# A graph network on one core: how far the upper half of the edges runs ahead of the lower half (LEAD 6 to 10)

## The chip, the cores and the metric

The kernel runs on one core of one Trainium2 chip. The metric is the device time of one execution in microseconds (us); the median of several runs is compared. Besides it there is a profile of one execution: a page of tables, and a trace that can be asked for single instructions.

The engines are named as the profile names them: PE (TensorE, matmuls; PEld is its weight loads), DVE (VectorE), ACT (ScalarE), POOL (GpSimd, which here issues the gathers) and SP (SyncE, which issues most other transfers).

## The reference

Two graph layers, each wrapped in a residual and a layer norm. The inputs are `x` of 6250 nodes x 256 features, and 100000 edges with source `src`, destination `dst` (sorted, and denser at low nodes, as it is 6250 u² for uniform u) and one of 8 types.

```python
# relational convolution, three times (L = 3)
for l in range(3):
    xr  = einsum('nd,rde->rne', x, W_rel[l])          # 8 types
    agg = segment_sum(xr[edge_type, src], dst)        # sum over the edges into a node
    x   = relu(agg + x @ W_root[l] + bias[l])
x = layernorm(x0 + x)
# attention over 4 heads of 64; only the first 6250 edges' weights reach the output
xt    = (x @ weight).reshape(-1, 4, 64)
alpha = softmax(leaky_relu(<xt[src], attn_l> + <xt[dst], attn_r>, 0.01), over heads)
tmp   = sum over heads of alpha[:n] * xt[dst[:n]]
out   = layernorm(x + tmp repeated for the 4 heads)
```

## The kernel before

**Tiles.** Edges are cut into 782 edge tiles of 128, nodes into 49 node tiles of 128. Edge tiles 0 to 35, the edges of the hottest 16 nodes, are handled by counting and by products of their own (`count`, `products`). Edge tiles 36 to 781 are taken in groups of up to four (`GT`), from high numbers to low: 188 groups per layer, 746 edge tiles.

**One group.** For each edge tile, POOL gathers 128 source rows from the table in memory into a message buffer (`gather`, line 499; pool `mp`, eight buffers, tile `msg`). DVE builds a one-hot of type and destination within a small window (`onehot`, line 483, four groups ahead). TensorE multiplies messages by the one-hot (`windows`, line 516, into the tile `pw`), and DVE adds the result into a sum `S` at a place read at run time (`add`, line 528). So `S` holds, for each node and type, the sum of source features.

**Node tiles.** When no later group reaches a node tile, its sums are final: `fold` wraps the ring's rim, `dense` multiplies by the weights (2 matmuls at line 580 and 16 at line 584, 6 matmuls after each group's windows, more where two tiles wait), `finish` (lines 598 to 619) adds the bias and writes the row of the next layer's table; in the third layer it adds the residual, normalizes and writes `y`. `clear` (line 593) zeroes the sums. In the third layer `logits` (line 632, copy at 634) follows two iterations after a finish.

**Two fronts.** Groups are split at edge tile 410 (`TM`). The upper half has a ring `S[0]` of four node tiles, the lower half `S[1]` of three, so that while one half's node tile is in its dense work, the other half's sums can be added. `Plan.order` merges both halves into one list, upper and lower in turn, with now and then two upper groups in a row, and a run of only lower groups at the end; `LEAD` sets how many. Node tile 13 is reached from both halves: its lower part is kept in `hold`, and added at line 827 when the upper half gets there.

**The order of everything.** The three layers are written under a manual schedule: each engine's queue has the order in which `layer` emits. The body of its loop over places in the list (shortened, a yield's worth of each helper at a time):

```python
for i in range(NG + 5):
    # prep step, counting, products, loads of rows for later node tiles
    msg = gather(i); vals = places(i); ohs.append(onehot(i + AHEAD))
    # logits of two iterations ago, finish and clear of node tiles just done
    wins = windows(i, msg, ohs.pop(0))
    # up to 6 dense matmuls per waiting node tile
    add(i, wins, vals)
    # second half of the prep step, transposes of rows, fold of node tiles just reached
```

In the third layer the attention's preparation (`prepare`, lines 723 to 758) begins at place 164 and takes one step for each lower group, and for each iteration after the last group. A step loads indices into a message buffer (line 723), compares the ones loaded before (line 730), builds a mask in another message buffer (line 736), and multiplies, selects and reduces (lines 745, 754, 758).

The next layer's gathers read the table that `finish` writes, so they wait for its last row.

Of the kernel before, what the change touches and what calls it, by code (L numbers as in the profile page):

```python
# [34 lines left out]
PIECE = 6  # L35
WB = 32
AHEAD = 4
LEAD = 6
GWIN = 256
GK = 8  # L40
GCW = 512
# [2 lines left out]
class Plan:  # L44
# [35 lines left out]
    def order(self):  # L80
# [3 lines left out]
        b = [[t for t in k if t < self.TM] for k in g if k[0] < self.TM]  # L84
        n = max(1, len(b) - LEAD)
        seq, k = [], 0
# [1289 lines left out]
```

## Time and profile before

| | us |
|---|---|
| median of 3 runs | 2975.68 |
| lowest and highest | 2972.78, 2980.37 |
| the profiled execution | 2972.97 |
| its span, first to last instruction | 2971.1 |
| mean granted TensorE clock | 0.939 of full |
| busy: PE, POOL, DVE, ACT | 2667.1, 2139.6, 1669.1, 458.5 |

An entry of the groups of instructions reads: line, engine, operation, output <- inputs, count | busy time and mean nanoseconds of one | idle time of the engine just before them, and what ended most of it. "issue" is time in which an engine waited for nothing that the profile shows. An entry of the waits reads: engine, line it stood before <- what it waited for: total us, times, longest us. An entry of the timeline reads: start in us from the span's start, duration in us, engine, line, operation, out <- in, how many instructions were merged, and in brackets the idle time before and what ended it. Matmuls in 32-bit floats appear as two records each.

### The profile page before, as it was taken

What the parts mean: (1) busy time and instruction counts of PE and PEld (TensorE: products, weight loads), DVE (VectorE), ACT (ScalarE), POOL (GpSimd) and SP (SyncE); (2) the same over time, 40 slices, a digit from 0 to 9 for tenths busy, and PEclk for the clock granted to TensorE, in tenths of its full rate; (3) what the DMA queues carried; (4) which work ended last, traced back from release to release, by engine and by line L of the source; (5) the groups of instructions that cost most, each with busy time, mean ns of one, the idle gap of its engine ahead of it and who ended that gap; (6) DMA issues with size and microseconds to landing.
All of it is one profiled execution on the core that took longest, in us unless ns stands there. A gap on an engine that the chain in (4) does not pass through costs nothing.

```text
span 2971.1 us, 45283 instructions
## 1 busy us (share of the span) xinstructions
PE 2667.1 (90%) x15710; PEld 2424.1 (82%) x15711; DVE 1669.1 (56%) x4094; ACT 458.5 (15%) x602; POOL 2139.6 (72%) x2254
## 2 busy tenths in 40 slices
PE   5999999989888799999988988779999999999985
PEld 4989888888777688998878877678888888888874
DVE  7645677764433555555444444356556665554778
ACT  2111111111001111111111110111111111110114
POOL 6777777777775777777777777577777777777741
PEclk9999999999988899999999997799999999998895
DMA  4444444445433444444444543344444444454534
GB/s 153 124 124 122 120 123 119 121 134 156 149 116 95 138 125 122 125 123 118 121 119 138 174 125 115 119 122 127 130 126 128 123 127 128 141 175 139 164 124 165
DMA packets 203053, 388.97 MB, mean 131 GB/s; under 512 B 42885, under 2 KB 128004, under 8 KB 202820
## 3 DMA queue, kind: packets, MB, share of 16 engines
q0 software_dynamic: 107424, 293.48, 33.8%
q1 hardware_dynamic: 92200, 89.76, 9.3%
q10 hardware_dynamic: 3196, 2.76, 0.3%
q8 instruction: 130, 2.13, 0.3%
q14 instruction: 103, 0.84, 0.1%
HBM read 360.18 MB, written 25.65 MB: 130 GB/s over the span
## 4 chain that ended last, share of the span: by engine, by line
PE 69%; POOL 9%; issue 7%; DVE 7%; DMA 5%; ACT 2%; DVEq 0%; ACTq 0%; POOLq 0%
PE pd L584 30%; PE pw L516 30%; POOL msg L499 9%; PE pd L580 4%; DMA msg<-x,idx 3%; DVE S L528 3%; DMA msg<-in_x_dram,idx 2%; PE pd L688 1%; PE pt L632 1%; PE pt L551 1%; ACT xT L554 1%; PE pd L659 1%; DVE st L1032 0%; DVE z L1020 0%; DVE oh L483 0%
## 5 line engine op out<-in xcount | busy, mean ns | idle before, releaser
L499 POOL DMA_INDIRECT msg<-x,idx x1492 | 1418.6, 951 | 504.8 <-issue 410.9
L516 PE MATMUL pw<-oh,msg 128*128 128x160 f32 (+22 forms) x8952 | 1304.7, 303 | 195.8 <-DMA msg<-x,idx 95.7
L516 PEld LDWEIGHTS pw<-oh,msg 128*128 128x128 f32 x8952 | 1248.4, 202 | 263.2 <-issue 104.6
L528 DVE TENSOR_TENSOR S<-S,pw 128x320 f32 (+22 forms) x2238 | 905.1, 404 | 986.7 <-PE pd L584 509.8
L584 PE MATMUL pd<-wr,S 128*128 128x256 f32 x4704 | 1106.7, 386 | 1.7 <-DVE S L528 1.4
L584 PEld LDWEIGHTS pd<-wr,S 128*128 128x128 f32 x4704 | 895.8, 194 | 116.8 <-DVE S L528 3.6
L499 POOL DMA_INDIRECT msg<-in_x_dram,idx x746 | 709.5, 951 | 236.2 <-issue 209.6
L483 DVE TENSOR_TENSOR oh<-iota,key 128x640 f32<-128x640 f32 (+23 forms) x564 | 364.0, 647 | 26.6 <-issue 15.3
L593 ACT ACTIVATE S<-S 128x2048 uint32<-128x2048 uint32 x150 | 285.1, 1900 | 0.1
L554 ACT COPY xT<-pt 128x256 f32<-128x256 f32 x195 | 72.2, 370 | 981.7 <-PE pt L551 969.7
L601 ACT ACTIVATE h<-pd 128x256 f32<-128x256 f32 x98 | 37.6, 383 | 929.8 <-DVE pd L598 747.8
L580 PE MATMUL pd<-wo,xT 128*128 128x256 f32 x588 | 168.8, 413 | 3.3 <-ACT h L601 3.3
L598 DVE TENSOR_TENSOR pd<-pd,bias_b 128x256 f32<-128x256 f32 x147 | 63.1, 430 | 172.5 <-PE pd L584 172.5
L580 PEld LDWEIGHTS pd<-wo,xT 128*128 128x128 f32 x588 | 110.3, 205 | 12.9 <-ACT h L601 3.7
L650 DVE TENSOR_SCALAR sel<-iota,hk 128x392 bf16<-128x392 f32 x138 | 80.4, 613 | 0.0
L615 ACT ACTIVATE rs<-mv,eps 128x1 f32<-128x1 f32 x49 | 14.4, 295 | 414.8 <-DVE mv L614 414.8
L688 PE MATMUL pd<-msg,A 128*128 128x256 f32 x294 | 73.0, 392 | 1.7 <-DMA msg<-x 1.7
L688 PEld LDWEIGHTS pd<-msg,A 128*128 128x128 f32 x294 | 57.0, 201 | 9.0 <-issue 2.1
L551 PE MATMUL pt<-ident,xin 128*128 128x128 f32 x294 | 57.8, 279 | 1.4 <-ACT xT L554 1.4
L632 PEld LDWEIGHTS pt<-w1x,xT 128*128 128x128 f32 x192 | 26.3, 198 | 35.4 <-ACT xT L554 35.4
L551 PEld LDWEIGHTS pt<-ident,xin 128*128 128x128 f32 x294 | 41.5, 146 | 12.6 <-ACT xT L554 2.4
L632 PE MATMUL pt<-w1x,xT 128*128 128x4 f32 x192 | 30.4, 264 | 23.6 <-ACT xT L554 23.6
(187 smaller groups left out, 641.9 us busy)
## 6 DMA issues: line engine op xcount, KB each, us to landing
msg<-x,idx POOLq DMA_INDIRECT x1492
x<-h SPq DMA_DIRECT2D x96, 128.0 KB
xin<-x SPq DMA_DIRECT2D x96, 128.0 KB
msg<-x SPq DMA_DIRECT2D x24, 512.0 KB
msg<-in_x_dram,idx POOLq DMA_INDIRECT x746
y<-yt SPq DMA_DIRECT2D x49, 128.0 KB
xin<-in_x_dram SPq DMA_DIRECT2D x48, 128.0 KB
msg<-in_x_dram SPq DMA_DIRECT2D x12, 512.0 KB
```

Of the source, the lines that this page charges most:

```text
L483: nc.vector.tensor_tensor(oh[:, :len(g), :w], iota[:, :w].unsqueeze(1).to_broadcast([P, len(g), w]), key[:, g[0]:g[-1] + 1].unsqueeze(2).t ...
L499: nc.gpsimd.indirect_dma_start(out=msg[:, q, :], out_offset=None, in_=table, in_offset=bass.IndirectOffsetOnAxis(ap=idx[:, t:t + 1], axis=0))
L516: nc.tensor.matmul(pw[:, k * w:(k + 1) * w], msg[:, q, k * P:(k + 1) * P], oh[:, q, :w], start=True, stop=True)
L528: ins = nc.vector.tensor_tensor(o, o, pw.rearrange("p (a b) -> p a b", b=W), ALU.add)
L551: nc.tensor.transpose(pt[:, k * P:(k + 1) * P], t[:, k * P:(k + 1) * P], ident)
L554: nc.scalar.copy(xT.rearrange("p k n -> p (k n)"), pt[:, :D])
L580: nc.tensor.matmul(pd[:, :D], xT[:, k], wo[:, k], start=(k == 0), stop=False)
L584: i = nc.tensor.matmul(pd[:, :D], s[:, k * R + r], wr[:, k, r], start=False, stop=(k == KC - 1 and r == R - 1))
L593: i = nc.scalar.memzero(cols(f, j))
L632: nc.tensor.matmul(pt[:, :H], yT[:, k], w1x[:, k, D + H:D + 2 * H], start=(k == 0), stop=(k == KC - 1))
L650: nc.vector.tensor_scalar(oh, iota[:, :NT * R], float(512 * n), hk[:, t:t + 1], op0=ALU.add, op1=ALU.is_equal)
L688: nc.tensor.matmul(ph[:, :D], A[:, j], t[:, n], start=(n == 0), stop=(j == js[-1]))
```

## The change

The constant `LEAD` goes from 6 to 10. In `Plan.order` it is subtracted from the number of lower groups to give the stretch over which the upper groups are spread.

```diff
 WB = 32
 AHEAD = 4
-LEAD = 6
+LEAD = 10
 GWIN = 256
```

## The prediction

> **What bounds the kernel now.** I read the page first: busy shares and the chain of waits.
>
> ```profile
> PE 2667.1 (90%) x15710; PEld 2424.1 (82%) x15711; DVE 1669.1 (56%) x4094; ACT 458.5 (15%) x602; POOL 2139.6 (72%) x2254
> PE 69%; POOL 9%; issue 7%; DVE 7%; DMA 5%; ACT 2%; DVEq 0%; ACTq 0%; POOLq 0%
> L499 POOL DMA_INDIRECT msg<-x,idx x1492 | 1418.6, 951 | 504.8 <-issue 410.9
> ```
>
> This looks like TensorE. The waits, and POOL's timeline at the end of the second layer, say otherwise:
>
> ```profile
> POOL msg L499 <- issue: 620.5, 2036, 0.6
> POOL msg L499 <- PE pw L516: 44.5, 109, 3.5
> ```
>
> ```profile
> 1897.61 0.94 POOL L499 DMA_INDIRECT msg<-x,idx  x1 [0.30 <-issue]
> 1898.86 0.95 POOL L499 DMA_INDIRECT msg<-x,idx  x1 [0.30 <-issue]
> 1918.16 0.95 POOL L499 DMA_INDIRECT msg<-x,idx  x1 [18.35 <-DMA x<-h]
> ```
>
> Nearly every gather follows the last by 1.25 us: 0.95 of work and 0.30 that waits for nothing. That gap doesn't count as busy, so "72%" hides a POOL with no free time. A layer has 746 gathers, 746 x 1.25 = 932.5 us. From first start to last end the timeline gives 936.5 (11.14 to 947.61), 934.8 (964.99 to 1899.81) and 952.9 (1918.16 to 2871.06). So layers one and two run at POOL's pace, 5.0 us for a group of four, with 4.0 and 2.3 us lost; layer three loses 20.4 us.
>
> Subtracting 5.0 us per group from the starts in layer three places that loss: 6.4 us at groups 63 to 84, 1.1 at group 144, 11.4 at groups 168 to 187, the rest in crumbs. Five of the gathers concerned:
>
> ```profile
> 2231.60 0.94 POOL L499 DMA_INDIRECT msg<-x,idx  x1 [2.85 <-PE pw L516]
> 2243.23 0.94 POOL L499 DMA_INDIRECT msg<-x,idx  x1 [1.71 <-PE pw L516]
> ...
> 2842.85 0.94 POOL L499 DMA_INDIRECT msg<-x,idx  x1 [1.97 <-PE pw L516]
> ...
> 2846.60 3.08 POOL L499 DMA_INDIRECT msg<-x,idx  x1 [0.30 <-issue]
> ...
> 2866.36 0.95 POOL L499 DMA_INDIRECT msg<-x,idx  x1 [1.62 <-DVE ga L758]
> ```
>
> The first two are a TensorE backlog that fills all eight message buffers. The others lie where the attention's preparation (L723 to L758) takes message buffers too; the 3.08 us gather overlaps the 2.29 us addition at L827.
>
> Between layers POOL idles 17.37 and 18.35 us, since the table must be written. The end of layer two on TensorE:
>
> ```profile
> 1900.80 2.84 PE L584 MATMUL pd<-wr,S 128*128 128x256 f32 x12
> 1903.48 1.87 PE L516 MATMUL pw<-oh,msg 128*128 128x32 f32 x16
> ...
> 1906.43 7.17 PE L584 MATMUL pd<-wr,S 128*128 128x256 f32 x32
> ```
>
> The last windows could start when the last gather has landed. For that I take a group at the start of layer two in the chain: gather start 982.75, windows 986.87, so 4.12 us. 1898.86 + 4.12 = 1902.98, and they start at 1903.48, 0.5 us late, behind dense work of node tile 13.
>
> **What the Trainium skill says.** "Perfetto Trace Analysis", Identifying the Most-Contended Engine: matmul busy time is a bad measure of the bound. The trace agrees: TensorE is 90% busy in layers that POOL paces. Same page, DMA Instruction — SWDGE (GPSIMD): such a slice ends with descriptor generation, not with the data. The trace agrees: 0.95 us of slice, 4.12 us to use. Same page, Optimization Strategy: repeated gaps on the engine that should be saturated can mean too few buffers; that fits POOL's waits in layer three. "SBUF — State Buffer", Who interferes with whom, infers that a two-input tensor_tensor leaves descriptor generation alone. Here the trace differs: the gather that meets L827 takes 2.71, 2.73 and 3.08 us in the three layers, instead of 0.95.
>
> **The change, part by part.** LEAD is used only in the order of groups, whose walk gives both lists. Nothing is added or removed: 94 upper and 94 lower groups, the same instructions, the same three-tile and four-tile rings. What moves: doubled upper groups rise from 5 places to 9; the last upper group goes from place 181 to 177; a run of lower groups closes the layer, 182 to 187 before, 178 to 187 after. SP's row loads, stores and the preparation's loads move with their iterations; rows are asked for three iterations (15 us) before they are turned, the preparation's one step before use. Weight loads stay at the layer's start. Semaphore waits stay where their instructions are.
>
> (1) *Gathers.* 746 per layer at 1.25 us in either order: 0 us. Not hidden by anything, merely unchanged.
>
> (2) *Ends of layers one and two.* Dense work of tiles 14 and 13 ends four iterations earlier, so nothing stands ahead of the last windows: -0.5 us in layer two, and -0.4 in layer one by the same sum (946.67 + 4.12 = 950.79 against 951.22). The rest of the 17 to 18 us is a chain through tile 0 that stays. Bounds: 0 and -1 each.
>
> (3) *TensorE ahead of POOL, layer three.* An upper tile costs 36 dense records of 0.217 us (12 in 2.6 us), a window record is 0.11 to 0.17 us by width, and logits add about 1.7 us per tile. Doubling upper groups earlier brings their dense work earlier. Summed over both lists, TensorE has up to 4.7 us more to do by places 56 to 71, 2.3 on average, and up to 5.6 by places 76 to 92; the lists agree again at the end. Buffers are full there (the 6.4 us), so POOL pays: I take +3 us, between average and first peak. Upper bound +5.6; lower -1.1 (all extra work falls into slack and the wait at group 144 goes). In layers one and two no such wait appears in POOL's timeline, thus 0; what hides the work is buffers not yet full. Without that cover they would pay up to 5.6 each.
>
> (4) *Preparation, layer three.* It takes 15 steps, one per lower group from place 164: nine in the alternation and six at 182 to 187 before; seven and eight (178 to 185) after. While a step both loads and selects, an iteration takes three message buffers; four such iterations follow each other before, six after. VectorE then sets the pace: its L730 starts at 2848.68, 2853.69, 2858.73 are 5.0 us apart, and 7.3 with a finished upper tile. Counting from the preparation's start (2761.72): before, place 178's step starts 69.0 us later and tile 0's dense work 119.0 us later (2880.70). After: 69.0 for the same fourteen iterations, 2.3 for L827, now ahead of 178, 25.2 + 2.3 for the five steps 178 to 182 with tile 14's finish, then the gathers of 185 to 187, 15.0, landing 2.9 (4.12 less 1.25), windows 1.9, and 0.6 of semaphores and addition: 119.2. The lighter 186 and 187 give back what the run costs: 0 us. Bounds: -4 (POOL's waits at 182, 183 and 187 all vanish: 0.73 + 1.69 + 1.32) and +8 (the slower rival).
>
> (5) *The end of layer three.* Tile 0's dense work ends at 2887.87, but VectorE finishes it only at 2889.33, because tile 13's logits (L632, then the copy at L634) come first. After the change those are done by place 185: -1.4 us. Bounds 0 and -1.5. The attention stage handles six late tiles in either order (0, 13 to 17 before; 0, 1, 13 to 16 after): 0 us.
>
> Sum: -0.9 + 3 + 0 - 1.4 = +0.7 us. The profiled execution took 2972.97 us (span 2971.1), which becomes 2973.7; the median of the runs is 2.7 above it, so I forecast 2975.68 + 0.7 = 2976.4 us.
>
> **The rivals.** *Slower: six three-buffer iterations in a row.* If POOL reaches place 178 less than two groups (10 us) ahead of its windows, each gather waits for a whole trip of the group two before: gathers 5.0, landing 2.9, windows 1.9, additions 1.0, select and reduce 2.9, together 13.7, or 6.85 us per group. For it: groups 182 to 183 and 183 to 184 are 6.69 and 7.13 us apart. Against: the next two are 5.03. Six at +1.85 are 11.1, and a second finish inside the run adds 2.3, against 5.1 lost there now: +8.3, with the +0.7 about +9: 2985 us.
>
> *Faster: TensorE is the bound after all.* Then 30 of the 36 dense matmuls of tiles 14 and 13 (60 x 0.217 = 13.0 us) leave each layer's last six groups: -39 us, 2937 us. For it: the chain is 69% PE. Against: POOL's unbroken 1.25 us rhythm, and only 0.5 us of lateness at the last windows. *Faster, by less:* the 11.4 us at groups 168 to 187 all go, since fewer steps lie in the alternation; with steps 2 and 5, -13.7, so 2962 us. Against: step 4's tighter run.
>
> That the change does nothing is excluded by the lists; that it moves nothing measurable is my forecast.
>
> **How the numbers follow.** About 0.3%, 8.9 us, is what a measurement can tell from no change. Forecast 0.80, slower rival 0.14, the faster ones 0.02 and 0.04. The steps' bounds, were all to fall one way, lie 9 below and 13 above the forecast; I hold the range at 2968 to 2988 us, which takes in the slower rival and leaves out the faster ones and the last microsecond of those stacks.
>
> **What would show it.** Right: first to last gather still about 936, 935 and 950 to 958 us; no POOL wait over 1 us in the first two layers; the boundary idles at 17 and 18 us; L827's long gather four groups earlier; larger TensorE waits near groups 56 to 72 of layer three; tile 0's finish directly after its dense work. Wrong: POOL waits in layers one or two, a run from 178 on paced at 6.5 us or more per group, or boundary idles that shrink by several microseconds.

## The result, and the profile after

The change makes the kernel slower. The median of five runs is 3003.9 us (2995.2 to 3005.9), against 2972.8 us (2967.4 to 2980.4) for five runs of the kernel before on the same chip. The ratio on record is 1.0093, with a 95% interval of 1.0077 to 1.0109 (the quotient of the two medians is 1.0105). The forecast was 2976.4 us and the range ended at 2988, so the prediction was wrong. The profiled execution of the kernel after has a span of 3002.1 us, 31.0 longer than before.

The page after, busy time and chain of waits:

```profile
PE 2687.1 (90%) x15710; PEld 2436.1 (81%) x15711; DVE 1667.3 (56%) x4094; ACT 458.0 (15%) x602; POOL 2136.3 (71%) x2254
PE 67%; POOL 10%; issue 8%; DVE 8%; DMA 5%; ACT 2%; DVEq 0%; SPq 0%; ACTq 0%; POOLq 0%
```

The instruction counts are those of before, record for record. Yet PE is busy 20.0 us longer (2667.1 before): the same matmuls ran more slowly. Nothing else on these lines says where.

POOL's timeline does. These are the last gather of layer two and the first of layer three, after:

```profile
1898.64 0.94 POOL L499 DMA_INDIRECT msg<-x,idx  x1 [0.30 <-issue]
1917.71 0.94 POOL L499 DMA_INDIRECT msg<-x,idx  x1 [18.13 <-DMA x<-h]
```

Layer three's first gather starts 0.45 us earlier than before (1917.71 against 1918.16). From there to the last gather:

| stretch of POOL's timeline, us | before | after |
|---|---|---|
| layer one, first to last gather | 936.5 | 935.6 |
| idle to layer two | 17.37 | 18.50 |
| layer two | 934.8 | 934.2 |
| idle to layer three | 18.35 | 18.13 |
| layer three | 952.9 | 986.5 |
| last gather to the end of the span | 100.0 | 97.8 |

All of the loss is in layer three, +33.6 us. The waits there, from the view of waits over 1915 to 2910 us of the kernel after (line, what it waited for: total, times, longest):

```profile
POOL msg L499 <- PE pw L516: 53.3, 52, 4.8
...
POOL msg L499 <- PE pt L551: 12.3, 8, 6.4
PE pd L688 <- DMA msg<-x: 9.4, 4, 2.7
```

In the same view of the kernel before:

```profile
POOL msg L499 <- PE pw L516: 24.7, 44, 3.5
```

POOL's waits for message buffers, which TensorE frees, more than double. The last line of the first fence is the one to follow. It says that TensorE itself waited, four times, in front of a matmul at line 688. That is in `products`, the separate treatment of the 16 hottest nodes, which the prediction didn't mention.

The groups of instructions of the page have the same line. First before, then after:

```profile
L688 PE MATMUL pd<-msg,A 128*128 128x256 f32 x294 | 73.0, 392 | 1.7 <-DMA msg<-x 1.7
```

```profile
L688 PE MATMUL pd<-msg,A 128*128 128x256 f32 x294 | 79.9, 418 | 21.2 <-DMA msg<-x 13.9
```

Same 294 records, 6.9 us more busy time, and 21.2 instead of 1.7 us of idle time ahead of them. These lines are of all three layers: 9.4 of the 21.2 us lie in layer three, the other 11.8 in layers one and two, which became no longer. So a wait here doesn't cost time by itself; why it does in layer three is taken up below.

How the matmuls slow down shows in the windows over 2520 to 2760 us of layer three (stretch, length, busy time and records of PE, PEld, DVE, ACT and POOL, granted TensorE clock, DMA share, GB/s), before and then after:

```profile
2520.00:2760.00 240.00, 224.53 (x1371) 204.59 (x1371) 130.41 (x347) 30.65 (x44) 180.66 (x192) 0.96 0.50 152
```

```profile
2520.00:2760.00 240.00, 214.88 (x1250) 193.41 (x1250) 122.08 (x321) 27.93 (x40) 169.48 (x180) 0.91 0.47 142
```

In the same 240 us POOL issues 180 gathers instead of 192: twelve fewer at 1.25 us are 15 us, near half of layer three's loss. TensorE starts 121 fewer records, is idle 9.7 us more, and its clock is 0.91 instead of 0.96.

### The profile page after: what moved, and what is told of

The parts are those of the page before. It is cut to its first block, busy times and chain, and to the rows that moved or that the text cites. A ratio compares the mean times of both kernels' runs of the same rounds, so it can differ in the third digit from the quotient of the medians.

```text
span 3002.1 us, 45291 instructions
## 1 busy us (share of the span) xinstructions
PE 2687.1 (90%) x15710; PEld 2436.1 (81%) x15711; DVE 1667.3 (56%) x4094; ACT 458.0 (15%) x602; POOL 2136.3 (71%) x2254
## 3 DMA queue, kind: packets, MB, share of 16 engines
q0 software_dynamic: 107424, 293.48, 34.1%
## 4 chain that ended last, share of the span: by engine, by line
PE 67%; POOL 10%; issue 8%; DVE 8%; DMA 5%; ACT 2%; DVEq 0%; SPq 0%; ACTq 0%; POOLq 0%
PE pw L516 30%; PE pd L584 28%; POOL msg L499 10%; PE pd L580 4%; DMA msg<-x,idx 3%; DVE S L528 3%; PE pd L688 2%; PE pt L551 1%; PE pt L632 1%; ACT xT L554 1%; DMA msg<-in_x_dram 1%; DVE sel L650 1%; DVE oh L483 0%; DMA msg<-x 0%; DVE st L1032 0%
## 5 line engine op out<-in xcount | busy, mean ns | idle before, releaser
L580 PEld LDWEIGHTS pd<-wo,xT 128*128 128x128 f32 x588 | 110.7, 205 | 14.7 <-ACT h L601 5.2
L688 PE MATMUL pd<-msg,A 128*128 128x256 f32 x294 | 79.9, 418 | 21.2 <-DMA msg<-x 13.9
L688 PEld LDWEIGHTS pd<-msg,A 128*128 128x128 f32 x294 | 60.0, 209 | 32.1 <-issue 10.8
```

The source lines that it names most:

```text
L580: nc.tensor.matmul(pd[:, :D], xT[:, k], wo[:, k], start=(k == 0), stop=False)
L688: nc.tensor.matmul(ph[:, :D], A[:, j], t[:, n], start=(n == 0), stop=(j == js[-1]))
```

## The late loads: how a change of order reaches them

`products` works in places too: at one place it emits a load of table rows (line 678, on SP's queue), at the next the matmuls that use it (line 688). `finish` puts the store of `y` (line 619) on the same queue, and that store waits until VectorE has normalized the row. This is SP's timeline of the kernel before, at the first such load, and the matmuls that use it:

```profile
2580.12 0.32 SPq L619 DMA_DIRECT2D y<-yt  x1
...
2581.21 0.37 SPq L678 DMA_DIRECT2D msg<-x  x1
```

```profile
2594.91 1.89 PE L688 MATMUL pd<-msg,A 128*128 128x256 f32 x8
```

The load goes out 13.7 us ahead of its use. Here too a store stands ahead of it, but that of the finish at place 126, four places earlier, so that TensorE still has the work of those places to do. After the change the finish is at place 129 and the load at 130 (SP, then PE):

```profile
2605.07 0.32 SPq L619 DMA_DIRECT2D y<-yt  x1
2605.75 0.92 SPq L678 DMA_DIRECT2D msg<-x  x2
```

```profile
2605.46 2.00 PE L516 MATMUL pw<-oh,msg 128*128 128x64 f32 x16 [0.82 <-DVE S L528]
2610.18 3.31 PE L688 MATMUL pd<-msg,A 128*128 128x256 f32 x8 [2.72 <-DMA msg<-x]
...
2621.31 1.89 PE L688 MATMUL pd<-msg,A 128*128 128x256 f32 x8
```

The load is held until the store has gone, and goes out 4.4 us ahead of the matmuls, for which TensorE stands idle 2.72 us. SP's own waits over 2560 to 2760 us tell the store from a lack of message buffers:

```profile
SPq L619 <- DVE yt L618: 141.1, 7, 26.4
...
SPq L678 <- PE pw L516: 1.2, 4, 0.5
```

The stores wait for VectorE, up to 26.4 us; the loads themselves wait hardly at all for TensorE to free a buffer.

After the wait the eight records take 3.31 us instead of 1.89. The Trainium skill, "TensorE: Matmul & The Clock Gate", Part 1: The HAM clock gate, says that an array that falls idle is throttled, and that sustained activity releases it; it puts the idle window at about 3.4 us. In this trace the granted clock is 1.00 over 2605.0 to 2610.1 us and 0.50 over 2612.0 to 2613.5, after a wait of 2.72 us, shorter than that window.

I call a load *late* if the order puts it directly behind a `finish` of the place before. With `LEAD` 6 one of the 13 loads is late (its matmuls are at place 139); with 10 there are four (matmuls at 131, 137, 145, 149). Before, TensorE waits at line 688 once, for 1.7 us; after, four times, for 9.4 us. The count and the waits don't pair off one to one. The wait before belongs to the last load, which has a line of its own (676), since VectorE must clear the rest of its buffer first; after the change it is there again, with 2.0 us. The late load of before is in time. Of the four after, that of 145 is in time too, and the other three are waited for, as the view of line 678 over 2500 to 2800 us has it under "who waited for it":

```profile
  PE pd L688: 7.4, 3
```

In layers one and two `finish` writes no `y`, but it stores the row `h` of the next table (line 602) on the same queue, and that store waits for ScalarE. The order there is the same, so the same loads are late. Layer one after the change, SP and then PE:

```profile
666.25 0.32 SPq L602 DMA_DIRECT2D x<-h  x1
666.75 1.10 SPq L678 DMA_DIRECT2D msg<-in_x_dram  x2
```

```profile
672.82 3.75 PE L688 MATMUL pd<-msg,A 128*128 128x256 f32 x8 [3.64 <-DMA msg<-in_x_dram]
```

At line 688 TensorE waits 7.3 us in layer one and 4.5 in layer two, and neither layer takes longer. The difference is how far behind TensorE is. Taking a group's gathers as usable 4.12 us after the start of its last one, as in the prediction, TensorE begins the windows of place 160 only 0.5 and 0.6 us later than that in layers one and two before the change, but 10.6 us later in layer three.

## The experiments

**Theory S** (late loads): the loss comes from TensorE's waits for loads held behind `y` stores. **Theory M** (message buffers): it comes from POOL, since `products` takes buffers of the ring from the gathers while TensorE is behind. **Theory R** (ratchet): each double upper group costs POOL a wait that is never won back, and they come earlier and larger. Ratios below are to the kernel before, with 95% intervals. The expectations name two rivals more: D, that double upper groups cost the same in every layer, and B, that TensorE's backlog alone is to blame, wherever it is paid. The table gives POOL's waits in layer three by place in the order, in us beyond 5.0 per group:

| places | before | after | own rows | moved products, LEAD 10 | early doubles |
|---|---|---|---|---|---|
| below 48 | 0.3 | 0 | 0.6 | 0 | 0.5 |
| 48 to 95 | 6.8 | 17.6 | 13.7 | 17.8 | 15.9 |
| 96 to 129 | 0.6 | 0.2 | 0.4 | 0.4 | 0.4 |
| 130 to 157 | 1.1 | 16.0 | 0.5 | 1.9 | 0 |
| 158 to 187 | 11.4 | 19.9 | 34.1 | 13.7 | 7.1 |
| sum | 20.2 | 53.7 | 49.3 | 33.8 | 23.9 |

Each column is one execution. Two kernels below repeat an order in layer three: `LEADS` (10, 10, 6) that of before, with 5.5, 6.8 and 13.4 us in the rows 48 to 95, 130 to 157 and 158 to 187, and (6, 6, 10) that of after, with 14.7, 18.0 and 19.0. So a difference of up to some 6 us in a row can be chance.

Eight kernels ran where the kernel before takes 3594 to 3599 us (*slow readings* below): POOL's gathers there show 199 to 225 us of waits whose releaser the trace doesn't name, and layer three can't be read. Six were run again where the kernel before takes some 2975 us; the two that were not stay open.

**Which layers.** `order` takes `lead`, and is called in each layer.

```diff
-LEAD = 6
+LEADS = (10, 10, 6)
```

> LEAD 10 in layers one and two, LEAD 6 in layer three. Theory M (message buffers): the whole loss of about 31 us lies in layer three, where TensorE is close to POOL's pace and other work takes message buffers; so this run is the kernel before again: 2971 to 2976 us, ratio 0.999 to 1.001, layer spans from first to last gather 935, 935 and 953 us. Theory S (SP's queue: product loads held behind the y stores) says the same, as y stores exist only in layer three. Rival D (doubled upper groups cost the same in every layer): 20 us of the 31 stay, 2993 us.

Measured: 2975.02 us, 1.0002 (0.9993 to 1.0011). With `LEADS = (6, 6, 10)`:

> LEAD 6 in layers one and two, LEAD 10 in layer three. Theories M and S: nearly all of the loss, 3001 to 3005 us, layer three 986 us from first to last gather. Rival D: a third of it, about 2983 us.

Measured: 3000.49 us, 1.0081 (1.0058 to 1.0104), four waits of TensorE for the products' loads in layer three, 9.0 us. In the first of the two kernels TensorE waits 8.7 and 4.3 us for such loads in layers one and two, and the run takes no longer. The loss is layer three's alone.

**Between.**

```diff
-LEAD = 6
+LEAD = 8
```

> LEAD 8 in all layers: seven doubled upper groups instead of five and nine, a last run of eight lower groups. Theory M, by a walk of TensorE's work: the excess ahead of places 56 to 72 and 120 to 134 is between those of 6 and 10, so 2980 to 2992 us. Theory S: it depends on whether a finish stands right ahead of place 130, so either near 2973 or near 2990, with no order in the three values. Rival D: half of the loss, 2988 us.

Measured: 2982.92 us, 1.0028 (1.0017 to 1.0039). That is in M's range, and what theory S expected, a time near one of the two ends and no order, did not come. Three loads are late by the count, and TensorE waits for these three, 3.5 us; but the profiled execution took 2976.98 us, the least of the ten, so its waits may be less than usual.

**Products with buffers of their own.** On `LEAD` 10; the room comes from one buffer of the one-hots.

```diff
-            t = mp.tile([P, GT, D], F32, name="msg")
+            t = hp.tile([P, GT, D], F32, name="rows4")
...
-            op = s.enter_context(tc.tile_pool(name="op", bufs=AHEAD + 2))
+            op = s.enter_context(tc.tile_pool(name="op", bufs=AHEAD + 1))
```

> LEAD 10, with the products' row tiles in one buffer of their own instead of the message buffers (room from one one-hot buffer fewer). Theory M: POOL's waits between groups 130 and 156 (16 us in all with LEAD 10, 1 us with LEAD 6) go almost wholly, so 2985 to 2991 us; the waits at groups 50 to 90 (18 us) and 167 to 187 (20 us) stay. Theory S: the loads stand behind the same y stores, TensorE still idles 9 us before line 688, so 3000 us or more. If one one-hot buffer fewer costs something, it shows in layers one and two, which stay at 935 us otherwise.

Measured: 3001.23 us, 1.0096 (1.007 to 1.0122). From the waits of layer three:

```profile
PE pd L688 <- DMA rows<-x: 10.3, 4, 3.9
```

POOL's waits at places 130 to 157 vanish, from 16.0 to 0.5 us, just as M says, and the kernel is no faster: 34.1 instead of 19.9 us come due at the preparation. TensorE begins the windows of place 160 28.7 us after their gathers could be used (counted as above), against 16.4 after the change and 10.6 before. The buffers only decide *where* POOL pays; what is paid is how far TensorE is behind. M falls as a cause. The late loads are still there: three are waited for, 8.5 us, and 1.9 us are the last load's.

**Moving the products by a place.** This changes which loads are late and no amount of work. By the count `LEAD` 10 goes from four to two (places 142, 156), `LEAD` 6 from one to four (134, 142, 146, 152), so S expects opposite signs. The numbers are again the places of the matmuls.

```diff
-HOT_AT = 130
+HOT_AT = 131
```

With `LEAD` 10:

> The kernel of e5 again (LEAD 10, HOT_AT 131), on a chip where the kernel before takes its 2975 us: the last chip needed 3599 us for it, and there nothing of layer three could be read. Theory S (SP holds a product load behind a y store): two late products instead of four, idle before line 688 from 9 us to 3 to 5, clock between 2520 and 2720 us 0.94 or more, 2985 to 2993 us. Rival B (TensorE's backlog alone): 2999 to 3004 us.

With `LEAD` 6:

> The kernel of e6 again (LEAD 6, HOT_AT 131), same reason. Theory S: four late products instead of one, idle before line 688 from 2 us to 7 or more, 2983 to 2995 us. Rival B: 2972 to 2977 us.

Measured: `LEAD` 10, 2987.12 us, 1.0048 (1.0031 to 1.0065); `LEAD` 6, 2985.26 us, 1.0032 (1.0023 to 1.004). From the waits of layer three, `LEAD` 10 and then `LEAD` 6:

```profile
PE pd L688 <- DMA msg<-x: 4.6, 1, 4.6
```

```profile
PE pd L688 <- DMA msg<-x: 8.1, 4, 3.3
```

`LEAD` 10 now has one wait at line 688, of 4.6 us, and has lost half of its excess, although `LEAD` is untouched. The wait is the last load's (156), which goes out 2.6 us after the store, when VectorE has cleared its buffer; the late load of 142 is in time, so no load of line 678 is waited for any more. `LEAD` 6 gets four waits, of 8.1 us, three of them (7.4 us) for late loads, and is slower than before. SP's timeline of the second, and the matmuls:

```profile
2610.26 0.32 SPq L619 DMA_DIRECT2D y<-yt  x1
2610.80 0.96 SPq L678 DMA_DIRECT2D msg<-x  x2
```

```profile
2615.38 1.99 PE L688 MATMUL pd<-msg,A 128*128 128x256 f32 x8 [1.87 <-DMA msg<-x]
```

It is the same picture as after the change: a store, the load close behind it, and TensorE waiting 4.6 us after the load went out. S holds in both directions, and both times lie in its ranges. It doesn't hold for all of the loss: 1.0048 without a wait for a load of line 678 leaves a rest. The slow readings of the two were 1.0027 and 1.0028.

**The `y` stores on another queue.**

```diff
-        nc.sync.dma_start(y[j * P:(j + 1) * P, :], yt)
+        nc.scalar.dma_start(y[j * P:(j + 1) * P, :], yt)
```

With `LEAD` 10:

> The kernel of e7 again (LEAD 10, y stores from ACT), same reason. Theory S: no wait of TensorE for product rows over 1 us, clock there 0.97, 2980 to 2988 us. Rival B: 2999 to 3004 us. If ACT's clears wait behind the stores: more than 3004 us.

With `LEAD` 6:

> The kernel of e8 again (LEAD 6, y stores from ACT), same reason. Theory S: 2968 to 2974 us. Rival B: 2972 to 2977 us. If ACT's order costs more than SP's: over 2977 us.

Measured: 2992.66 us, 1.0054 (1.0038 to 1.0071), and 2980.19 us, 1.0013 (1.0001 to 1.0025). Each has one wait at line 688, of 1.9 us, the last load's. So the held loads are freed, and with `LEAD` 10 a good part of the loss goes. But the move has a price of its own: ACT's line 593, which clears the sums, now waits for VectorE behind the store. Layer three's waits, `LEAD` 10:

```profile
ACT S L593 <- DVE yt L618: 18.9, 18, 1.1
...
PE pd L688 <- DMA msg<-x: 1.9, 1, 1.9
```

The waits went as S says; the times are above its ranges (2988 and 2974 us at most), and with `LEAD` 6 the time is where ACT's order was to cost more than SP's. So these two runs can't size S. Their slow readings were 1.0046 and 0.9998.

**The first half of the order alone.** Doubles as early as with `LEAD` 10 up to the middle, then as spread out as with `LEAD` 6, so that the last upper group is at place 181 as before; products moved as above, which leaves one late load.

```diff
-            while k < len(a) and k * n <= i * len(a):
+            while k < len(a) and k <= (i * len(a) / 84 if i <= 45 else len(a) - (len(a) - 45 * len(a) / 84) * (88 - i) / 43):
...
-HOT_AT = 130
+HOT_AT = 131
```

> The kernel of e13 again (LEAD 10's pace up to lower group 45, strictly in turn after, HOT_AT 131, one late product), for a chip where the kernel before takes 2975 us. Theory R (TensorE's peaks of early dense work are charged to POOL): POOL waits of 16 to 18 us between groups 48 and 95, few after, 2983 to 2989 us. Rival: only the late part of the order costs, 2973 to 2978 us.

Measured: 2974.04 us, 1.0005 (0.9995 to 1.0016). Two of POOL's gathers near place 64 of layer three:

```profile
2238.22 0.94 POOL L499 DMA_INDIRECT msg<-x,idx  x1 [2.60 <-PE pw L516]
...
2251.55 0.94 POOL L499 DMA_INDIRECT msg<-x,idx  x1 [3.32 <-PE pw L516]
```

The early waits are all there, 15.9 us at places 48 to 95 against 17.6 after and 6.8 before, and the run takes no measurably longer: the later ones fall from 12.5 (places 130 on, before) to 7.1 us, and at place 160 TensorE is 3.5 us late where before it is 10.6. Upper groups that are done early leave TensorE less to do later. R, by which such waits are never won back, falls. The slow reading of this kernel was 1.0025.

**The late half alone** (`84` and `88` exchanged, with 39 for 43, and `HOT_AT = 131`):

> Only the second half of LEAD 10: LEAD 6's pace up to lower group 45, then faster, so that the last upper group stands at 177 (doubles at 30, 61, 90, 105, 116, 129, 142, 153, 166); HOT_AT 131, two late products (138, 142). Theory R: waits between groups 48 and 95 about 7 us as before; one late product more and the longer last run cost 2 to 6 us, 2976 to 2982 us. Rival (late doubles and the run of ten lower groups are what costs): 2985 us or more.

Measured only as a slow reading: 3599.66 us, 1.0022 (1.0005 to 1.0039).

**A smaller lead** (`LEAD = 3`):

> LEAD 3 in all layers: three doubled upper groups, one late product (139), a last run of three lower groups. Theories R and S: waits between groups 48 and 95 at or under the 7 us of LEAD 6, no late product more; but tiles 14 and 13 reach their dense work nearer to each layer's end, which may hold the last windows by some 3 to 5 us per layer: 2970 to 2985 us. If nothing is held at the ends, 2966 to 2972 us, faster than both.

Measured only as a slow reading: 3603.08 us, 1.0017 (0.9997 to 1.0036). Neither tells the theories apart.

**Less work on TensorE.** On `LEAD` 10; type 0 is left out of layer three's dense work, some 42 us of matmuls.

```diff
-            for r in range(R):
+            for r in range(1 if final else 0, R):
```

> The kernel of e15 again (LEAD 10, HOT_AT 130, relation 0 left out of layer three's dense work, 42 us less of TensorE), same reason. Theories R and S: layer three takes 934 to 945 us from first to last gather, the run 2950 to 2962 us. Rival (POOL's waits come from the buffers' order, not from TensorE's lag): layer three stays above 965 us.

Measured: 2968.18 us, 0.9988 (0.9973 to 1.0002), 6 us above the expected range; the slow reading was 1.0012. The profiled execution took 2963.11 us. From the waits of layer three:

```profile
POOL msg L499 <- PE pw L516: 16.4, 42, 1.7
...
PE pd L688 <- DMA msg<-x: 10.5, 4, 2.7
```

All four late loads are there, three of them waited for as after the change (7.9 of the 10.5 us), and POOL doesn't feel them: layer three takes 944.0 us from first to last gather, and its waits beyond the pace are 1.4 us at places 48 to 95, 0 at 130 to 157 and 9.3 in the preparation. So a late load costs only because TensorE in layer three has no slack to win it back, as it has in layers one and two. That is the condition that S needs.

## Why the prediction was wrong, point by point

**What bounds the kernel.** For layers one and two the reading was right: with `LEAD` 10 there alone the ratio is 1.0002, and POOL keeps its 1.25 us rhythm. Layer three was read by the same rule, as POOL's pace plus a few waits. Its TensorE is in fact behind for most of the layer already before the change, by 28.5 us on average at places 48 to 95 and still by 10.6 at place 160. There TensorE's idle time and clock are on the path. Setting each group's start of windows against the time when its gathers can be used would have shown it.

**Step 1, gathers.** Right: 746 per layer at 1.25 us.

**Step 2, ends of layers one and two, -0.9.** The gathers took 0.9 and 0.6 us less, but the idle times that were to shrink went up 1.1 and down 0.2. PE's timeline at the end of layer two, after:

```profile
1901.46 3.60 PE L516 MATMUL pw<-oh,msg 128*128 128x32 f32 x16 [1.33 <-DMA msg<-x,idx]
1904.87 2.05 PE L580 MATMUL pd<-wo,xT 128*128 128x256 f32 x4
1906.72 7.49 PE L584 MATMUL pd<-wr,S 128*128 128x256 f32 x32
```

As foretold nothing stands ahead of the last windows, so TensorE waits 1.33 us for the data. But the windows then take 3.60 us where the same 16 took 1.87 before, and the next four 2.05 instead of 1.11 us. The clock was low already: in each of the last four groups TensorE had idled 0.8 to 2.0 us ahead of the windows, and its granted clock from 1890 to 1905 us is 0.50. Before, with dense work in between, it is 1.00 from 1900 to 1906 us.

**Step 3, TensorE ahead of POOL, +3.** POOL's waits at places 48 to 95 rose by 10.8 us, beyond the upper bound of 5.6. That POOL pays at each peak of TensorE's lateness, the work of one not being given back before the next, is the likely reason and not shown. The early doubles show that such waits cost the end nothing where the later order gives them back. So the number was too small, and it isn't a cost by itself.

**Step 4, preparation, 0, between -4 and +8.** The waits at places 158 to 187 rose by 8.5 us. The run at the end isn't their main place: two gathers, at 168 and 170, account for 6.4 of it, more than they waited before. In POOL's timeline after:

```profile
2791.66 0.95 POOL L499 DMA_INDIRECT msg<-x,idx  x1 [4.79 <-PE pw L516]
...
2807.94 0.95 POOL L499 DMA_INDIRECT msg<-x,idx  x1 [6.36 <-PE pt L551]
```

They wait for TensorE, which arrives at the preparation late (16.4 us at place 160 against 10.6). At places 174 to 187, where the slower rival was to act, the waits rose by 2.3 us (8.8 against 6.5). That rival had the sign, but at most this much of the 33.6 us can be its mechanism.

**Step 5, end of layer three, -1.4.** Measured -2.2, from the last gather to the end: the right way, and beyond the bound of -1.5.

**The step that failed** is "SP's row loads, stores and the preparation's loads move with their iterations". The products' loads stay at fixed places, one place ahead of their use. As the other things on SP's queue move past them, `y` stores come to stand directly ahead of loads. The sum had no term for it. Moving the products by one place measures it: 1.0093 against 1.0048, 0.45% or 13 us (by the two intervals some 7 to 20; the medians, of different chips, are 16.8 apart), and in the other direction 0.32%, 9.5 us, at `LEAD` 6. In the waits for late loads themselves it is 7.4 us of TensorE's time both times; the rest of the 13 and the 9.5 us is put down to the slower matmuls afterwards, which no run separates. And it needed the misreading of layer three: in layers one and two, where POOL does set the pace, 11.8 us of waits for the products' loads cost nothing.

**What stays open.** With the products moved, `LEAD` 10 is still 0.48%, some 14 us, behind, and layer three 13.7 us longer than before (966.6 against 952.9). The wait for the last load, 4.6 instead of 1.7 us, is in it. By the table 11.0 of the 13.6 us that POOL waits longer lie at places 48 to 95. The early doubles wait about as much there (9.1 us more than before), but get 5.4 us back from place 130 on, and here 3.1 us are added. So the rest should lie in the second half of the order, which doesn't give the early waits back: the upper groups end at place 177 instead of 181, and dense work falls earlier, just as TensorE reaches the preparation. This is argued, from single executions: the kernel with the late half alone has only a slow reading.

## What to carry to other kernels

When an order of emission is changed, list every queue and look for what does *not* move with it: a load emitted one step ahead of its use is safe only while nothing that waits is emitted just before it on the same queue, or while the engine that uses it has time to spare. Where two engines take turns in being late, the waits of the first are no sum of costs: removing POOL's waits moved them on, and doubling them early cost nothing measurable. Read the bound stage by stage, and where an engine is behind, count a microsecond of its idle time in full, and the slower work after it too.

## What the runs showed of the hardware

- TensorE slowed down after some short waits: 3.31 instead of 1.89 us for eight records after 2.72 us of idle time, with the granted clock going from 1.00 to 0.50. It didn't after every one: with `LEAD` 6 and the products moved, 1.87 us of idle time were followed by 1.99 us for eight records and a clock of 1.00. Over layer three's 2520 to 2760 us the mean clock is 0.91 after the change, 0.95 with the products moved as well, and 0.96 before.
- SP issued its transfers in the order in which they were emitted, so which engine issues a transfer matters. The Trainium skill, "DMA: Bandwidth & Descriptors", Issuing engines are not separate DMA queues, says that issuing from several engines saves only the time of the sequencer. Here a store that waited for VectorE held a load behind it, and with the stores issued by ACT TensorE's waits at line 688 went from 9.4 to 1.9 us: it saved waiting, and put 18.9 us of it on ACT.
- The same kernel took some 2975 us at some times and 3594 to 3599 us at others, and the ratios measured there (1.0012 and 1.0025 for the two repeated kernels whose ratios here are 0.9988 and 1.0005) don't carry over. One chip number, 4, stands with readings of either kind, so it isn't shown that the chip makes the difference.
